# Loading the weights on the rows' queue, a later look at the redo count, and logit columns made by TensorE

## The chip, the cores and the metric

The kernel runs on one core of a Trainium2 chip. The metric is device time in microseconds for one execution; before the change the median of three runs is 2867.93 us (2864.26 to 2868.86). A profile of one execution tells when each instruction started, how long it ran, and what ended the wait before it.

The engines by their names in the profile: PE (TensorE, products; PEld is its loading of weights), DVE (VectorE), ACT (ScalarE), POOL (GpSimd), SP (SyncE, which here issues transfers). Each engine takes its instructions in the order in which they were written, and an instruction that waits holds up those behind it on that engine.

## The reference

Two graph layers over 4096 nodes with 256 features, in float32. Cut to what matters:

```
h   = relu(layernorm(x));  hw = (h @ W) in 4 heads of 64
src = hw . a[:64],  dst = hw . a[64:]              # one logit each per node and head
out = softmax over neighbours of leakyrelu(src_i + dst_j), times hw
x   = x + layernorm(out)
X   = relu(layernorm(x))
for n in 0, 1:
    P  = softmax(X W1' W2' (X W3')')                # 4096 x 4096
    A  = P cut to the smallest set of entries that holds 0.9 of each row, renormalised
    Xf = R Xf;  X = A X                             # R: the graph's adjacency with self loops, normalised
    Z += Xf U1[n]' + X U2[n]'
result = x + layernorm(relu(layernorm(x)) + Z)
```

## The kernel before, in words

The 4096 rows are 32 blocks of 128. The kernel runs in stages.

**Prologue.** `X` holds all rows. SP loads block 0 (L197), blocks 1 to 3 (L201) and then seven groups of four (L195). ACT's queue loads the vector `a` copied to all 128 partitions (`a_r`, L198), the two halves of W into the tile `wx` (L200), then three tiles of weights for the attention layer (L204 to L206). `wx` has 256 columns of W and 8 more. Those 8 are W times the two halves of `a`, per head, so that one product of a row block with `wx` yields both `hw` and the logits. Before the loop over blocks, DVE makes these columns with four multiplications (L571) and four sums (L573), two of each for each half of W. Between the halves it measures mean and variance of blocks 1 to 3 (`measured`, L149 and L150), and after them those of blocks 4 to 7. POOL makes scale and shift from them (`steps`, L141 to L144): for block 0 alone, then for blocks 1 to 3 together, then by fours. `opened` applies them on ACT (`hb`, L240), `turned_rows` transposes on PE (L247), `multiplied` copies the transposed rows to `hT` (ACT, L251) and multiplies with `wx` (PE, L254).

`turn_of(b)` then works one turn for each block: it transposes block b+1, multiplies block b, opens block b+2, measures block b+8, and splits earlier blocks into bfloat16 parts for the masked products that follow (L395). These products are the first long stage of PE; they end near 789 us. The stage after them is the first graph product (L622), with the first attention step's preparation woven in.

**Attention steps.** For each of the two steps n, block b's probabilities `e` are searched by DVE for the cut, and masked (L1022). PE transposes them in eight groups of four (`turn`, L1088, copied to `eT` by ACT at L1090) and sums the chosen rows (`gather`, L1096). `attend` interleaves these eight groups with other work from a table, `beside`, which maps a group number to functions called after that group. `turn` takes its PSUM tile from a pool of two (`tp`).

At the end of a step the kernel must know whether any row's search failed. `questioned` makes the flags after the last block's masking (DVE, L1164 to L1176). `looked` calls `counted`, which sums the flags with two small PE products (L878, in two `tp` tiles) and reads them out on DVE (L880 to L884), and `chosen`, which sorts the numbers of the blocks to redo (DVE, L1192 to L1201). `number` reads the count into a register of every engine (L1187). `repaired` then redoes blocks if the count is above zero. In the kernel before, `looked` stands after group 6 of block 30, and `number` in `beginning`, after group 0 of block 31. In step 0, the last block also carries the loads for the second graph product: `both_weights` (L717) after group 1, `begin` (rows and adjacency, L455 and L474) after group 2.

All waits between engines are semaphores that the compiler of the program places. Transfers from SP and ACT share eight semaphores in turn, so a transfer also waits until the eighth one before it has landed.

Of the kernel before, what the change touches and what calls it, by code (L numbers as in the profile page):

```python
# [11 lines left out]
F32 = mybir.dt.float32  # L12
# [11 lines left out]
AX = mybir.AxisListType  # L24
# [32 lines left out]
def gat_then_top_p_diffusion(  # L57
# [79 lines left out]
    def steps(mv, n, pool, rs=None, nmr=None):  # L137

        if rs is None:
            rs, nmr = (pool.tile([P, n], F32, name=x, bufs=2) for x in (f"rs{n}", f"nmr{n}"))  # L140
        nc.gpsimd.tensor_scalar(rs, mv[:, :, 1], EPS, None, ALU.add)  # L141
        nc.gpsimd.tensor_tensor(rs, rs, mhalf.to_broadcast([P, n]), ALU.pow)
        nc.gpsimd.tensor_scalar(nmr, mv[:, :, 0], -1.0, None, ALU.mult)
        nc.gpsimd.tensor_tensor(nmr, nmr, rs, ALU.mult)  # L144
        return rs, nmr
# [16 lines left out]
    with tc.tile_pool(name="l0", bufs=1) as l0, tc.tile_pool(name="l0s", bufs=2) as l0s, tc.tile_pool(name="l0o", bufs=1) as l0o:  # L162
# [25 lines left out]
        pro = SimpleNamespace(read=lambda: None, hb={}, pt={}, hT={}, pm={}, uv={}, scales={})  # L188
        with tc.manual_schedule(engines=every | {ET.SP}):
            wx = rp.tile([P, KC, D + 2 * H], F32, name="wx", tag="ar", bufs=4)  # L190
            a_r, w1_s, w2_s, w1_r, sT = (rp.tile(sh, F32, name=x, tag="hl", bufs=5) for x, sh in (
                ("a_r", [P, 2 * HD]), ("w1_s", [P, KC, DA]), ("w2_s", [DA, DA]), ("w1_r", [DA, KC, P]), ("sT", [P, P])))

            def block_rows(g):
                nc.sync.dma_start(X[:, ts(g, 4), :], x[ts(g, 4 * P), :].rearrange("(b p) d -> p b d", p=P))  # L195

            nc.sync.dma_start(X[:, 0, :], x[:P, :])  # L197
            nc.scalar.dma_start(a_r, bass.AP(tensor=a.tensor, offset=a.offset, ap=[[0, P], [1, 2 * HD]]))  # L198
            for k in range(KC):
                nc.scalar.dma_start(wx[:, k, :D], w[ts(k, P), :])  # L200
            nc.sync.dma_start(X[:, 1:4, :], x[P:4 * P, :].rearrange("(b p) d -> p b d", p=P))  # L201
            for g in range(1, NB // 4):
                block_rows(g)
# [19 lines left out]
            def measured(b):  # L223
                if b < NB:
                    if b % 4 == 0:
                        pro.mv = l0s.tile([P, 4, nc.vector.BN_AGGR_DIM], F32, name="mv4")
                    moments_of(pro.mv[:, b % 4, :], X[:, b, :])
                    if b == 0:
                        pro.first = [l0s.tile([P, 4], F32, name=f"{x}4") for x in ("rs", "nmr")]
                        steps(pro.mv[:, :1], 1, l0s, *(t[:, :1] for t in pro.first))  # L230
                    if b == 3:
                        steps(pro.mv[:, 1:], 3, l0s, *(t[:, 1:] for t in pro.first))
                    elif b % 4 == 3:
                        pro.scales[b // 4] = steps(pro.mv, 4, l0s)

            def opened(b):
                if b < NB:
                    rs, nmr = pro.scales[b // 4] if b > 3 else pro.first
                    hb = pro.hb[b] = l0s.tile([P, D], F32, name="hb", tag="ob")
                    nc.scalar.activation(hb, X[:, b, :], AF.Relu, scale=rs[:, b % 4:b % 4 + 1], bias=nmr[:, b % 4:b % 4 + 1])  # L240

            def turned_rows(b):
                if b < NB:
                    hb = pro.hb.pop(b)
                    pt = pro.pt[b] = in_bank(3 + b % 2, [P, KC, P])
                    for k in range(KC):
                        nc.tensor.transpose(pt[:, k, :], hb[:, ts(k, P)], ident)  # L247
# [317 lines left out]
        rest.update({5 + i: lambda i=i: factors(i) for i in range(2)})  # L565
        with tc.manual_schedule(engines=every):
            measured(0)
            for k in range(KC):
                for i in range(2):
                    pr = uvs[3 + i][:, :, 0, :HD]  # L570
                    nc.vector.tensor_mul(pr, wx[:, k, :D].rearrange("p (h d) -> p h d", h=H),  # L571
                                         a_r[:, None, ts(i, HD)].to_broadcast([P, H, HD]))
                    nc.vector.reduce_sum(wx[:, k, ds(D + i * H, H)], pr, axis=AX.X)  # L573
                if k == 0:
                    for b in range(1, 4):
                        measured(b)
            for b in range(4, 8):
                measured(b)
            opened(0)
            turned_rows(0)  # L580
            opened(1)
            for b in range(NB):
                turn_of(b)
            read(NB - 1)
            weighed(NB - 1)
            mask_stage(1)
            signed(3)
            sign_stage(2)
            for n, (k, p) in enumerate(todo):
                if n > 0 and p == 0:  # L590
                    later.extend(evacuate(k - 1))
                sign_stage(n + 3)
                mask_stage(n + 2)
                if n == 0:
                    products(k, p, ms[n], range(5))
                    spread_all()
# [589 lines left out]
    def number(R, total):  # L1186
        return nc.values_load(total[1], engines=everyone, min_val=0, max_val=6 * P * NB)  # L1187
# [159 lines left out]
    for n in range(STEPS):  # L1347
# [4 lines left out]
        with tc.manual_schedule(engines=every):  # L1352
# [50 lines left out]
            def beginning():  # L1403
                normal(blocks[NB - 3])
                gathered(blocks[NB - 2])
                finish(blocks[NB - 2])
                finish_scale(blocks[NB - 2])
                R.count = number(R, R.undone)

            beside = {NB - 2: {5: last_chosen, 6: looked}, 0: dict(zip((0, 1, 3, 5, 6), S.turned))}  # L1410
            for b in range(NB - 1):
                chosen_kept(b)
                if b + AHEAD < NB:
# [6 lines left out]
                polished(blocks[NB - 3])  # L1420
                finish_rows(blocks[NB - 2])

            beside = {0: beginning, 3: earlier}
            if n + 1 < STEPS:
                second = hop_of(n + 1)
                beside.update({1: both_weights, 2: lambda: begin(second, 4), 5: lambda: split(second, 2), 6: lambda: (split(second, 4), own(second, 4))})
            attend(r, cur, None, beside)
            for m in range(second.begun if n + 1 < STEPS else 0):
                for s in range(KC):
# [37 lines left out]
```

## Time and profile before

| what | value |
|---|---|
| median of the runs | 2867.93 us |
| profiled execution, its own time | 2866.9 us |
| its span | 2865.1 us |
| PE busy | 2795.3 us, 98% |
| DVE busy | 2169.1 us, 76% |
| ACT busy | 1918.8 us, 67% |
| first product with `wx` (L254) | 14.12 us |
| first masked product (L395) | 88.58 us |
| count of step 0 on PE (L878) | 1776.60 us |
| count of step 1 on PE (L878) | 2834.86 us |
| last store issued (L1304) | 2861.26 us |

A timeline line gives start, duration, engine, source line, instruction, what it writes and reads, and shape; the brackets hold how long its engine was idle before it and what released it. A line "x8" merges eight instructions of a kind. PE shows two records for one float32 product, so the four products of a `gather` are eight records. Lines L1 to L1466 are those of the kernel before.

### The profile page before, as it was taken

To read this page: it belongs to the slowest core of one execution; us is meant where nothing else is said; L and a number is where in the kernel's file an instruction comes from. 1 tells how busy PE (TensorE), PEld (TensorE's weight loads), DVE (VectorE), ACT (ScalarE), POOL (GpSimd) and SP (SyncE) were. 2 spreads that over 40 slices of the span, in tenths; PEclk is the share of its full clock that TensorE was granted. 3 is DMA by queue.
4 is the path that set the end of the run, shared out by engine and by line. 5 is a ranking of instruction groups with operands and counts; after the bars stand their busy time and mean duration, and the time that the engine had idled before them with its cause. 6 is when DMAs were issued, how large, how long until landed. Compare 5 with 4: busy or idle time off the path is not lost. (4 is left out here: it accounts for less than half of the span.)

```text
span 2865.1 us, 51492 instructions
## 1 busy us (share of the span) xinstructions
PE 2795.3 (98%) x18777; PEld 2436.3 (85%) x18777; DVE 2169.1 (76%) x5069; ACT 1918.8 (67%) x3065; POOL 865.7 (30%) x1811
## 2 busy tenths in 40 slices
PE   5999999999999999999999999999999999999998
PEld 4899999999978788888888888667778888888886
DVE  8867868678554385888888887333665999999996
ACT  7876886879543636788878874233627788777882
POOL 6402121010000121222332231000204756666664
PEclk8999999999999999999999999999999999999999
DMA  8969596696376783000000001767991111111110
GB/s 192 243 250 204 204 234 188 229 198 222 133 236 196 240 298 95 20 20 20 27 20 20 20 20 56 229 200 236 327 340 43 31 41 31 31 31 33 39 29 25
DMA packets 190394, 376.48 MB, mean 131 GB/s; under 512 B 18224, under 2 KB 143152, under 8 KB 186032
## 3 DMA queue, kind: packets, MB, share of 16 engines
q1 hardware_dynamic: 146832, 275.05, 29.9%
q0 software_dynamic: 21504, 83.89, 12.3%
q10 hardware_dynamic: 21792, 14.11, 1.6%
q8 instruction: 152, 2.49, 0.4%
q14 instruction: 114, 0.93, 0.1%
HBM read 305.55 MB, written 113.57 MB: 146 GB/s over the span
## 5 line engine op out<-in xcount | busy, mean ns | idle before, releaser
L1096 PE MATMUL acc<-X,eT 128*128 128x256 f32 x4096 | 973.6, 383 | 3.4 <-ACT eT L1090 2.8
L1096 PEld LDWEIGHTS acc<-X,eT 128*128 128x128 f32 x4096 | 739.1, 190 | 111.5 <-ACT eT L1090 31.5
L395 PE MATMUL acc<-ut,m 128*128 128x195 bf16 (+1 forms) x8192 | 698.7, 246 | 2.2 <-DVE st L412 1.7
L395 PEld LDWEIGHTS <-m 128*128 128x128 fp8e4 x8192 | 695.9, 97 | 4.9 <-DVE st L412 2.2
L369 ACT ACTIVATE g<-sr,d_big 128x1024 uint8<-128x1024 f32 x448 | 472.6, 1136 | 3.4 <-DVE m L375 3.4
L911 ACT ACTIVATE e<-mm,nm 128x1024 f32<-128x1024 f32 x256 | 286.1, 1117 | 200.1 <-PE mm L728 198.8
L1090 ACT COPY eT<-tp 128x512 f32<-128x512 f32 x512 | 296.5, 580 | 87.5 <-PE tp L1088 87.4
L997 DVE MAX8 cand<-big 128x8 f32<-128x228 f32 (+1 forms) x1152 | 348.2, 380 | 0.0
L622 PE MATMUL mm<-ar,hl 128*128 128x512 f32 x844 | 340.7, 407 | 5.9 <-ACT ob L502 1.3
L979 DVE SCALAR_TENSOR_TENSOR big<-e,c 128x4096 f32<-128x4096 f32 x58 | 261.9, 4516 | 97.5 <-POOL c L964 67.1
L622 PE MATMUL acc<-ar,hl 128*128 128x512 f32 x844 | 328.6, 392 | 2.3 <-DVE stage L632 1.3
L935 POOL TENSOR_TENSOR sums<-sums 128x2 f32<-128x2 f32 x64 | 12.6, 197 | 1030.9 <-ACT void L918 1030.9
L1088 PE MATMUL tp<-ident,e 128*128 128x128 f32 x2048 | 306.0, 272 | 0.8 <-DVE e L1022 0.8
L1088 PEld LDWEIGHTS tp<-ident,e 128*128 128x128 f32 x2048 | 254.8, 140 | 60.2 <-PE acc L1106 1.2
L375 DVE TENSOR_TENSOR m<-g,ax 128x512 uint32<-128x512 uint32 x256 | 180.8, 706 | 109.9 <-PE acc L395 91.4
L1022 DVE SCALAR_TENSOR_TENSOR e<-e,found 128x4096 f32<-128x4096 f32 x58 | 259.1, 4468 | 0.0
L918 ACT ACTIVATE void<-e,c1x 128x2048 int8<-128x2048 f32 x128 | 257.4, 2011 | 0.8 <-ACT stage L651 0.8
L918 ACT ACTIVATE void<-e,c 128x2048 int8<-128x2048 f32 x128 | 257.5, 2012 | 0.0
L728 PE MATMUL mm<-kT,qT 128*128 128x512 f32 x512 | 198.4, 468 | 2.9 <-ACT e L911 1.9
L376 DVE TENSOR_TENSOR m<-m,ax 128x512 uint32<-128x512 uint32 x256 | 180.4, 705 | 26.0 <-PE acc L395 0.9
L622 PEld LDWEIGHTS mm<-ar,hl 128*128 128x128 f32 x844 | 158.6, 188 | 44.9 <-issue 5.0
L622 PEld LDWEIGHTS acc<-ar,hl 128*128 128x128 f32 x844 | 158.6, 188 | 39.9 <-issue 4.9
(302 smaller groups left out, 3507.4 us busy)
## 6 DMA issues: line engine op xcount, KB each, us to landing
ar<-adj_d SPq DMA_DIRECT2D x211, 512.0 KB, 4.7
adj_d<-ax POOLq DMA_DIRECT2D x32, 2048.0 KB, 7.7
ut<-uv_d SPq DMA_DIRECT2D x60, 784.0 KB, 5.6
aru<-adj_d SPq DMA_DIRECT2D x45, 512.0 KB, 4.6
ax<-in_adj_t_dram POOLq DMA_DIRECT2D x32, 512.0 KB, 17.4
x<-xf_d SPq DMA_DIRECT2D x78, 128.0 KB, 4.9
xf<-xft_d SPq DMA_DIRECT2D x64, 128.0 KB, 2.3
sr<-s_d SPq DMA_DIRECT2D x15, 512.0 KB, 4.9
```

Source lines behind the costliest of these rows:

```text
L369: nc.scalar.activation(g[:, c, :], shared[k].sr, AF.Relu, scale=BIG, bias=d_big[:, h, j:j + 1])
L395: nc.tensor.matmul(shared[k].acc[i][:, t, :cols], m[t][:, c, ts(i, P)], shared[k].ut[j // QUARTER][:, j % QUARTER, t, :cols], start=(j == ...
L622: nc.tensor.matmul(A.acc[c][s], A.hl[m][:, t, ts(s, P)], A.ar[m][:, ts(c, 512)], start=(j == 0 and t == 0), stop=(j == NB - 1 and t == 1))
L728: nc.tensor.matmul(pm[:, h, :], q[t], kT[:, ds(h * (N // 2) + c * 512, 512)], start=(t == 0), stop=(t == 1))
L911: nc.scalar.activation(ev[:, :, c, :], r.pm[c], AF.Exp, bias=r.nm, accum_out=r.sums[:, c // 2, c % 2:c % 2 + 1])
L918: nc.scalar.activation(void, r.e[:, ts(h, N // 2)], (AF.Relu, AF.Sign)[i], bias=r.c1, scale=-1.0, accum_out=r.sums[:, h, 2 + i:3 + i])
L979: nc.vector.scalar_tensor_tensor(big, r.e, r.c3, r.e, ALU.is_le, ALU.mult, accum_out=r.low3)
L997: nc.vector.max(cand[:, s, :], big[:, edges[s]:edges[s + 1]])
L1022: nc.vector.scalar_tensor_tensor(r.e, r.e, r.t, r.e, ALU.is_ge, ALU.mult, accum_out=kept)
L1088: nc.tensor.transpose(pt[:, i, :], r.e[:, ts(4 * g + i, P)], ident)
L1090: nc.scalar.copy(eT, pt)
L1096: nc.tensor.matmul(r.acc[:, 0, :], eT[:, i, :], cur[:, j, :], start=(j == 0), stop=(j == NB - 1))
```

## The change

It has three parts. W is loaded in one transfer on SP's queue, behind block 0 and ahead of blocks 1 to 3, and ACT's queue loads `a` into a tile `spots` instead: zero but for the entries of `a`, each put at its own row of W' and in the column of its head and half. The 8 columns of `wx` are then made by PE: four transposes of W's quarters, copied by DVE to `w_t`, and four products of `w_t` with `spots`, copied by DVE into `wx`. Blocks 1, and 2 with 3, get their scales separately. Finally `looked` goes to group 1 of block 31, the reading of the count to group 4 (`asked`), and `both_weights` to group 2, ahead of `begin`.

```diff
-            a_r, w1_s, w2_s, w1_r, sT = (rp.tile(sh, F32, name=x, tag="hl", bufs=5) for x, sh in (
-                ("a_r", [P, 2 * HD]), ("w1_s", [P, KC, DA]), ...
+            w_t, w1_s, w2_s, w1_r, sT = (rp.tile(sh, F32, name=x, tag="hl", bufs=5) for x, sh in (
+                ("w_t", [P, KC, KC, P]), ("w1_s", [P, KC, DA]), ...
             nc.sync.dma_start(X[:, 0, :], x[:P, :])
-            nc.scalar.dma_start(a_r, bass.AP(tensor=a.tensor, offset=a.offset, ap=[[0, P], [1, 2 * HD]]))
-            for k in range(KC):
-                nc.scalar.dma_start(wx[:, k, :D], w[ts(k, P), :])
+            spots = l0.tile([P, KC, 2, H], F32, name="spots")
+            nc.vector.memset(spots, 0.0)
+            for h in range(H):
+                nc.scalar.dma_start(spots[ds(h * HD % P, HD), h * HD // P, :, h],
+                                    bass.AP(tensor=a.tensor, offset=a.offset, ap=[[1, HD], [HD, 2]]))
+            nc.sync.dma_start(wx[:, :, :D], w.rearrange("(k p) d -> p k d", p=P))
             nc.sync.dma_start(X[:, 1:4, :], x[P:4 * P, :].rearrange("(b p) d -> p b d", p=P))
...
-                        steps(pro.mv[:, :1], 1, l0s, *(t[:, :1] for t in pro.first))
+                    if b < 2:
+                        steps(pro.mv[:, ds(b, 1)], 1, l0s, *(t[:, ds(b, 1)] for t in pro.first))
                     if b == 3:
-                        steps(pro.mv[:, 1:], 3, l0s, *(t[:, 1:] for t in pro.first))
+                        steps(pro.mv[:, 2:], 2, l0s, *(t[:, 2:] for t in pro.first))
...
             measured(0)
+            pt = in_bank(0, [P, KC, KC, P])
             for k in range(KC):
-                for i in range(2):
-                    pr = uvs[3 + i][:, :, 0, :HD]
-                    nc.vector.tensor_mul(pr, wx[:, k, :D].rearrange("p (h d) -> p h d", h=H),
-                                         a_r[:, None, ts(i, HD)].to_broadcast([P, H, HD]))
-                    nc.vector.reduce_sum(wx[:, k, ds(D + i * H, H)], pr, axis=AX.X)
-                if k == 0:
-                    for b in range(1, 4):
-                        measured(b)
+                for c in range(KC):
+                    nc.tensor.transpose(pt[:, k, c, :], wx[:, k, ts(c, P)], ident)
+            nc.vector.tensor_copy(w_t, pt)
+            opened(0)
+            turned_rows(0)
+            pm = in_bank(1, [P, KC, 2 * H])
+            for k in range(KC):
+                for c in range(KC):
+                    nc.tensor.matmul(pm[:, k, :], w_t[:, k, c, :], spots[:, c].rearrange("p t h -> p (t h)"),
+                                     start=(c == 0), stop=(c == KC - 1))
+            for b in range(1, 4):
+                measured(b)
+            nc.vector.tensor_copy(wx[:, :, D:], pm)
             for b in range(4, 8):
                 measured(b)
-            opened(0)
-            turned_rows(0)
             opened(1)
...
                 finish_scale(blocks[NB - 2])
+
+            def asked():
                 R.count = number(R, R.undone)
 
-            beside = {NB - 2: {5: last_chosen, 6: looked}, 0: ...}
+            beside = {NB - 2: {5: last_chosen}, 0: ...}
...
-            beside = {0: beginning, 3: earlier}
+            beside = {0: beginning, 1: looked, 3: earlier, 4: asked}
             if n + 1 < STEPS:
                 second = hop_of(n + 1)
-                beside.update({1: both_weights, 2: lambda: begin(second, 4), 5: ..., 6: ...})
+                beside.update({2: lambda: (both_weights(), begin(second, 4)), 5: ..., 6: ...})
```

More of the change, by code (lines that the diff above doesn't have):

```diff
@@ L190, in gat_then_top_p_diffusion @@
             wx = rp.tile([P, KC, D + 2 * H], F32, name="wx", tag="ar", bufs=4)
-            a_r, w1_s, w2_s, w1_r, sT = (rp.tile(sh, F32, name=x, tag="hl", bufs=5) for x, sh in (
-                ("a_r", [P, 2 * HD]), ("w1_s", [P, KC, DA]), ("w2_s", [DA, DA]), ("w1_r", [DA, KC, P]), ("sT", [P, P])))
+            w_t, w1_s, w2_s, w1_r, sT = (rp.tile(sh, F32, name=x, tag="hl", bufs=5) for x, sh in (
+                ("w_t", [P, KC, KC, P]), ("w1_s", [P, KC, DA]), ("w2_s", [DA, DA]), ("w1_r", [DA, KC, P]), ("sT", [P, P])))
             def block_rows(g):
@@ L1407, in beginning @@
                 finish_scale(blocks[NB - 2])
+            def asked():
                 R.count = number(R, R.undone)
-            beside = {NB - 2: {5: last_chosen, 6: looked}, 0: dict(zip((0, 1, 3, 5, 6), S.turned))}
+            beside = {NB - 2: {5: last_chosen}, 0: dict(zip((0, 1, 3, 5, 6), S.turned))}
             for b in range(NB - 1):
@@ L1421, in earlier @@
                 finish_rows(blocks[NB - 2])
-            beside = {0: beginning, 3: earlier}
+            beside = {0: beginning, 1: looked, 3: earlier, 4: asked}
             if n + 1 < STEPS:
                 second = hop_of(n + 1)
-                beside.update({1: both_weights, 2: lambda: begin(second, 4), 5: lambda: split(second, 2), 6: lambda: (split(second, 4), own(second, 4))})
+                beside.update({2: lambda: (both_weights(), begin(second, 4)), 5: lambda: split(second, 2), 6: lambda: (split(second, 4), own(second, 4))})
             attend(r, cur, None, beside)
```

## The prediction

> **What bounds the kernel now.** I read first the page's busy times, then the busy time by stretches, then the timeline around the three places that the diff touches: the first 16 us, the end of the first attention step, and the last 40 us.
>
> ```profile
> PE 2795.3 (98%) x18777; PEld 2436.3 (85%) x18777; DVE 2169.1 (76%) x5069; ACT 1918.8 (67%) x3065; POOL 865.7 (30%) x1811
> ...
> 20.00:30.00 10.00, 6.93 (x34) 4.88 (x32) 9.46 (x30) 9.21 (x27) 7.50 (x11) 1.00 0.39 86
> 30.00:40.00 10.00, 7.12 (x28) 5.35 (x28) 9.86 (x30) 8.67 (x26) 8.33 (x15) 0.83 1.02 175
> ...
> 100.00:120.00 20.00, 20.00 (x238) 20.00 (x237) 18.93 (x26) 18.62 (x22) 10.36 (x11) 1.00 0.99 196
> ```
>
> The first line is the page's (engine, busy us, share); the others give, by stretch, PE, PEld, DVE, ACT and POOL busy time, then clock, DMA share and GB/s. PE is busy 98% of the span, and from 100 us almost without a gap. So an edit pays only where PE waits, or where the work ahead of PE's long run (the prologue, bound by DVE at 9.5 to 9.9 us of each 10) starts late. Time gained before such a stretch is kept, because what follows is a queue of work and no fixed date.
>
> The timeline of the first 16 us (start, duration, engine, line, what; in brackets the idle time before and what ended it):
>
> ```profile
> 4.33 0.43 DVE L149 BATCH_NORM_STATS2 st<-X 128x6 f32<-128x256 f32 x1 [4.33 <-DMA X<-in_x_dram]
> ...
> 7.69 0.43 DVE L571 TENSOR_TENSOR sr<-wx,a_r 128x256 f32<-128x256 f32 x1 [2.72 <-DMA wx<-in_w_dram]
> ...
> 8.24 0.60 ACT L240 ACTIVATE hb<-X,nmr,rs 128x256 f32<-128x256 f32 x1 [6.21 <-DMA X<-in_x_dram]
> ...
> 11.05 0.31 POOL L141 TENSOR_SCALAR rs<-mv 128x3 f32<-128x3 f32 x1 [4.53 <-DVE mv L150]
> ...
> 12.98 0.60 ACT L240 ACTIVATE hb<-X,nmr,rs 128x256 f32<-128x256 f32 x1 [4.14 <-POOL nmr L144]
> ...
> 14.12 1.97 PE L254 MATMUL b<-wx,hT 128*128 128x264 f32 x4
> ```
>
> PE's first product (14.12) hangs on hb of row block 1 (12.98), that on POOL's factors (11.05), and those on DVE having measured blocks 1 to 3, which it did behind four of the L571/L573 instructions.
>
> The timeline at the ends of the two attention steps:
>
> ```profile
> 1773.44 1.89 PE L1096 MATMUL acc<-X,eT 128*128 128x256 f32 x8
> 1776.60 0.22 PE L878 MATMUL tp<-undone,ones 128*1 128x32 f32 x2 [1.27 <-DVE undone L1176]
> ...
> 2829.65 1.89 PE L1096 MATMUL acc<-X,eT 128*128 128x256 f32 x8
> 2834.86 0.27 PE L878 MATMUL tp<-undone,ones 128*1 128x32 f32 x2 [3.32 <-DVE undone L1176]
> ...
> 2835.17 3.44 PE L1096 MATMUL acc<-X,eT 128*128 128x256 f32 x8
> ```
>
> PE stands at the count (L878) until DVE has the flags: 1.27 and 3.32 us. After the longer stand the next eight products take 3.44 instead of 1.89 us.
>
> **What the Trainium skill says.** "TensorE: Matmul & The Clock Gate", section "What's actually happening": PE falls to half clock after an idle window of about 3.4 us; the 3.44 us group fits that (the short stand shows no slow group). "DMA: Bandwidth & Descriptors", section "Rules for kernel authors": an access whose last dimension is not contiguous becomes one descriptor per element; each of the four spread loads is 128 pieces of 4 bytes, and no row of this trace has such. Same page, "Issuing engines are not separate DMA queues": changing the queue saves only issue time. The trace differs here: from 5 to 6 us SP's queue has 81% of DMA time and ACT's 17%, and wx, issued on ACT at 1.21, lands 6.4 to 7.3 us later. Position decides.
>
> **The prologue.** Removed: eight DVE instructions of 0.39 to 0.43 us, 3.4 us, and the 64 KB row of a. Added: a small memset, four loads of 0.5 KB, four PE transposes, four PE products with 8 columns, a DVE copy of 128x512 (0.69 us, the L782 row) and one of 128x16 (about 0.15), and four short POOL operations, as block 1 gets factors of its own.
>
> Arrival. SP's queue has moved 0.13 MB at 3 us, 0.41 at 5, 0.66 at 6, 0.93 at 7. Transfers are signalled 1.3 us (block 0) to 2.4 us (blocks 1 to 3) after their bytes. W is now second: 0.39 MB, so bytes at 4.9 and signal at 6.2 to 7.3; I take 6.7. Blocks 1 to 3 go behind it: 0.77 MB, bytes at 6.4, signal at 7.7 to 8.8 (before: 7.79); I take 8.4. ACT still issues the key weights ahead of hb, and by the built kernel's waits the last of them (L206 before, issued at 7.80) waits for blocks 1 to 3: hb of block 0 starts at about 8.85 instead of 8.24.
>
> Two paths to the first product.
> - By block 1: W at 6.7, four cold transposes (two took 0.69 at 8.89) to 7.9, DVE copy to 8.65, block 1 measured (0.43+0.18) by 9.25, POOL's four steps (5.06 to 6.52 for one column, 1.46) to 10.7, hb at 10.8; before, the product came 1.14 after hb's start: 11.95.
> - By the columns: hb of block 0 to 9.45, its transposes to 10.2, then the spread products queued behind them. The nearest row, L827 (65 columns, 16 records in 1.73 us warm), gives 0.108 a record, so 0.9 us warm and 1.7 cold for eight records; I take cold: 11.9. Then DVE's copy to 12.1 and block 1's transposes to 12.6.
>
> The later one sets it: 12.6 instead of 14.12, 1.5 us. Bounds 0 (W as late as before) and 3 (early W, warm PE). Blocks 4 to 7 are measured behind the column copy, until 14.2; their factors are ready at 16.2, hb of block 4 by 16.85, and PE, 1.5 us earlier, wants it at 17.8: hidden, but with only 1 us of room. The rows of later blocks come behind 0.25 MB more, with many us to spare. The small loads must land by about 10; issued from 1 to 3 us and nearly empty, I put them at 5 to 7.
>
> **The count.** The two L878 products move from before the last eight products of block 30 to after the second gather of block 31; flags are then long ready (2834.5 against PE there at about 2838.7). Block 31's masked rows are ready at 2830.9 and PE now asks for them at 2833.6, so no new stand there. What it costs: L878 takes a pair of the two rotating buffers that the transposes use, so the next transposes wait until DVE has read the count out. Before, L878 started at 1776.60 and that reading ended at 1777.31; before, eight products covered it. Now nothing does: 0.9 us each step with the pair itself.
> First step: PE's weight loads are free at 1774.93, the gather came at 1776.81: 1.9 - 0.9 = 1.0 us. Last step: free at 2831.14 and, unhindered, 1.60 later at the next group (2832.74), where it was 2838.23: 5.5 - 0.9 = 4.6 us.
>
> The reading of the count into registers moves from the last block's group 0 to group 4 on all engines. "DMA: Bandwidth & Descriptors", "Latency and other measured facts", prices a tensor load at about 0.6 us; here L1187 takes 0.3 to 0.6. On PE it lies under queued products (before, no gap at the transposes behind it, 2842.47; 1.9 us of cover), on POOL before the last factors (6.0 us idle), on DVE in 14.1 us of idle time. On SP it was ahead of the second weights and hop loads (u issued at 1782.41 after 0.9 us); now it is behind them, and ahead of an aru load that waits for PE until 1798 anyway. If these covers were gone it would be 0.6 us per step. The chain after the first step (xa stored, rows loaded, first ar) starts at the last block's end and moves along. DVE's second half for block 30 now follows the count; its store has over 10 us.
>
> Sum: 1.5 + 1.0 + 4.6 = 7.1 us. The profiled execution, 2866.9 with a span of 2865.1, would be 2859.8 and 2858.0; the median of the runs, 2867.93, is 1.0 above it, so I forecast 2860.8.
>
> **Rivals.**
> - The prologue gives nothing: W and the rows arrive together late, or hb of block 4 is short of its 1 us. For it: only 1 us of cover, and bytes that stay the same. Against: block 1 no longer waits for 2 and 3. 5.6 us, 2862.3.
> - The wait returns at the transposes behind L878: if DVE is behind there by 2 us per step instead of 0.9, and PE stays cool at the end (1.5), 3.5 us are lost: 2864.3. Against: DVE's last work before it ends at about 2836, 2.5 us before PE comes.
> - Slower: the columns of the logits are now rounded otherwise; if a single row then fails the top-p test, a block is redone. Nothing is redone before: nothing runs after the last store at 2861.26. Price from rows: 8 column groups of about 0.6 (ACT, half of 1.117 each), six passes or half passes over 4096 columns (about 14), eight groups of 2.17: at least 36 us, about 2900. It decides from the first row on.
> - The move does nothing, if PE needs the masked rows as late as the flags: excluded by 2830.9 against 2834.5.
>
> **Numbers.** Forecast 0.64, first rival 0.20, second 0.09, slower 0.04, nothing 0.03. Here 0.2% is 5.7 us, about what a measurement of this kernel can tell from no change. The forecast's own range is 3.5 to 10.5 us of gain, most of it beyond 5.7; the first rival is split about evenly; the others are same or slower. Faster 0.68, same 0.26, slower 0.06. The range takes in the first two rivals and the bounds of the prologue: 2856 to 2866.
>
> **What will show it.** L878 with no wait on DVE, the group after it at 1.9 us, and a short gap (0.5 to 1.0) at the transposes behind; the last gather near 2847.5 instead of 2854.6; first L254 near 12.6 and not 14.1, and the first L395 (88.58) as much earlier. I am wrong if the small loads land after 10 us, if the gain at the first L254 is gone at the first L395, or if new work follows the last store.

## The result and the profile after

The kernel after takes 2859.86 us (median of 8 runs, 2857.15 to 2860.89), the kernel before beside it 2865.49 us (8 runs, 2863.33 to 2868.86). The medians differ by 5.6 us. The ratio estimated from all runs is 0.9977, with a 95% interval of 0.9968 to 0.9987: 6.6 us faster, between 3.7 and 9.2. The profiled execution takes 2860.89 us with a span of 2859.1, against 2866.9 and 2865.1 before.

The first line of the kernel after's page, and its busy times by stretches (columns as in the prediction):

```profile
PE 2798.3 (98%) x18789; PEld 2438.7 (85%) x18789; DVE 2167.1 (76%) x5064; ACT 1919.8 (67%) x3065; POOL 870.5 (30%) x1815
...
30.00:40.00 10.00, 7.66 (x31) 5.85 (x32) 9.86 (x30) 8.66 (x26) 8.51 (x13) 0.84 0.91 181
100.00:120.00 20.00, 20.00 (x238) 20.00 (x237) 18.17 (x25) 18.64 (x20) 8.40 (x9) 1.00 0.91 239
```

PE has 12 more records and 3.0 us more to do; its gaps shrank. What bounds each stretch is as before: DVE, busy 90 to 99% of each 10 us from 20 to 90 us, then PE. The timeline of the first 16 us of the kernel after:

```profile
2.96 0.43 DVE L149 BATCH_NORM_STATS2 st<-X 128x6 f32<-128x256 f32 x1 [2.07 <-DMA X<-in_x_dram]
...
4.76 1.09 PE L575 MATMUL b<-ident,wx 128*128 128x128 f32 x4 [4.76 <-DMA wx<-in_w_dram]
...
6.24 0.60 ACT L244 ACTIVATE hb<-X,nmr,rs 128x256 f32<-128x256 f32 x1 [4.22 <-DMA X<-in_x_dram]
...
9.31 1.42 PE L582 MATMUL b<-spots,w_t 128*128 128x8 f32 x6 [1.50 <-DMA spots<-in_a_dram]
...
11.09 2.10 PE L258 MATMUL b<-wx,hT 128*128 128x264 f32 x4
```

The first product with `wx` (now L258) starts at 11.09 instead of 14.12. The weights are there at 4.7, and even block 0, whose load was not touched, comes 1.4 us earlier. What comes last is a small load: PE waits 1.50 us for `spots`. The first masked product (now L399) starts at 85.59 instead of 88.58, so in these two traces the 3 us are kept until there.

The timeline at the ends of the attention steps (L1096 is now L1104, L878 is L886, the transposes L1096):

```profile
1771.31 3.62 PE L1104 MATMUL acc<-X,eT 128*128 128x256 f32 x16
1781.05 0.22 PE L886 MATMUL tp<-undone,ones 128*1 128x32 f32 x2
1781.82 0.66 PE L1096 MATMUL tp<-ident,e 128*128 128x128 f32 x4 [0.49 <-DVE ns_i_u L892]
...
2827.58 3.62 PE L1104 MATMUL acc<-X,eT 128*128 128x256 f32 x16
2837.32 0.22 PE L886 MATMUL tp<-undone,ones 128*1 128x32 f32 x2
2838.14 0.66 PE L1096 MATMUL tp<-ident,e 128*128 128x128 f32 x4 [0.55 <-DVE ns_i_u L892]
```

The sixteen products run through (3.62 us) where PE stood 1.27 and 3.32 us. L886 waits for nothing; behind it PE stands 0.49 and 0.55 us until DVE has read out the sums. Matched instruction by instruction, the traces show the lead of the kernel after over the kernel before: ahead of the end of step 0 it is 2.1 us and behind it 3.0; ahead of the end of step 1 it is 2.1 and behind it 6.4. So the ends gave 0.85 and 4.4 us. With the 3.0 of the prologue that is 8.2; the spans differ by 6.0. So about 2 us net were lost in between, above all in the two graph products (985 to 1005 and 2025 to 2112 us), where nothing was changed.

### The profile page after: what moved, and what is told of

Its sections match the earlier page's. It is cut to its first block, busy times and chain, and to the rows that moved or that the text cites. A ratio compares the mean times of both kernels' runs of the same rounds, so it can differ in the third digit from the quotient of the medians.

```text
span 2859.1 us, 51521 instructions
## 1 busy us (share of the span) xinstructions
PE 2798.3 (98%) x18789; PEld 2438.7 (85%) x18789; DVE 2167.1 (76%) x5064; ACT 1919.8 (67%) x3065; POOL 870.5 (30%) x1815
## 5 line engine op out<-in xcount | busy, mean ns | idle before, releaser
L1104 PE MATMUL acc<-X,eT 128*128 128x256 f32 x4096 | 971.7, 382 | 3.4 <-ACT eT L1098 2.8
L1104 PEld LDWEIGHTS acc<-X,eT 128*128 128x128 f32 x4096 | 738.2, 190 | 111.2 <-ACT eT L1098 31.7
L399 PE MATMUL acc<-ut,m 128*128 128x195 bf16 (+1 forms) x8192 | 698.7, 246 | 1.9 <-DVE st L416 1.4
L399 PEld LDWEIGHTS <-m 128*128 128x128 fp8e4 x8192 | 695.9, 97 | 4.6 <-DVE st L416 1.8
L1096 PE MATMUL tp<-ident,e 128*128 128x128 f32 x2048 | 306.1, 272 | 1.9 <-DVE ns_i_u L892 1.0
L1096 PEld LDWEIGHTS tp<-ident,e 128*128 128x128 f32 x2048 | 254.8, 140 | 61.2 <-DVE ns_i_u L892 1.3
```

What stands on the lines that cost most here:

```text
L399: nc.tensor.matmul(shared[k].acc[i][:, t, :cols], m[t][:, c, ts(i, P)], shared[k].ut[j // QUARTER][:, j % QUARTER, t, :cols], start=(j == ...
L1096: nc.tensor.transpose(pt[:, i, :], r.e[:, ts(4 * g + i, P)], ident)
L1104: nc.tensor.matmul(r.acc[:, 0, :], eT[:, i, :], cur[:, j, :], start=(j == 0), stop=(j == NB - 1))
```

## The experiments

The theory I started with (A): each gain is local, is kept, and they add up. The rival (B): the graph products take an earlier start back, because their transfers set the pace there. (In the second one DMA moves 348 GB/s at a share of 0.99, in the first 216 GB/s at 0.70; PE is busy 96% of both.) Further questions were what makes the start of the prologue earlier, and what still holds it.

**The two parts alone.** The first kernel undoes the count's part (the reading of the count goes back into `beginning`), the second makes only that.

```diff
 # e1, against the kernel after
-            beside = {NB - 2: {5: last_chosen}, ...
+            beside = {NB - 2: {5: last_chosen, 6: looked}, ...
-            beside = {0: beginning, 1: looked, 3: earlier, 4: asked}
+            beside = {0: beginning, 3: earlier}
-                beside.update({2: lambda: (both_weights(), begin(second, 4)), ...
+                beside.update({1: both_weights, 2: lambda: begin(second, 4), ...
 # e2: the same lines, the other way round, against the kernel before
```

> The kernel after with the count's part undone: only the prologue differs from the kernel before. Theory A (each gain is local and is kept): the first L258 product starts near 11.1 us as in the kernel after (14.12 before), the first attention group (L399) about 3.0 us earlier than before, and the count still stands 1.3 and 3.3 us for DVE with a slow group after the second stand; time 3.0 us below the kernel before, ratio 0.9990. Theory B (the graph products, whose stretches move 340 to 350 GB/s and are bound by DMA, take an earlier start back): the 3.0 us shrink to about 2 behind the first graph product (near 1000 us) and to 1 or less behind the second (near 2110), time 0 to 1.5 us below. The prediction's own step was 1.5 us, with a first product at 12.6.

> The kernel before with the count's part alone: the prologue is that of before. Theory A: first product at 14.1 us, no shift until the end of attention step 0; there 0.85 us gained, at the end of step 1 another 4.4, time 5.2 us below the kernel before, ratio 0.9982; the group of sixteen L1096 products around the count at 3.6 us both times. Theory B: the 0.85 us of step 0 is gone behind the second graph product, time 4.4 below. If the slow group of before was not caused by the 3.32 us stand, a group near 3.4 for eight products stays and the gain at the last step is about 2.8 instead of 4.4.

Measured beside the same runs of the kernel before (2866.31 us): the prologue alone 2864.2, ratio 0.9993 (0.9985 to 1.0002), so 2.0 us; the count alone 2861.78, ratio 0.9985 (0.9978 to 0.9991), so 4.3 us. Together 6.3, where the kernel after has 6.6. The sum fits, within intervals 3.7 to 4.9 us wide. The first interval holds no change too: that the prologue's part gains rests on the traces below and is not shown by the times.

At the end of step 1 the kernel with the prologue alone has the stand of before, but not what followed it. Timelines of this kernel, and of the kernel before in a second run (its expectation comes further down):

```profile
2833.53 0.22 PE L886 MATMUL tp<-undone,ones 128*1 128x32 f32 x2 [3.32 <-DVE undone L1184]
...
2833.74 1.99 PE L1104 MATMUL acc<-X,eT 128*128 128x256 f32 x8
```

```profile
2834.58 0.27 PE L878 MATMUL tp<-undone,ones 128*1 128x32 f32 x2 [3.30 <-DVE undone L1176]
...
2834.89 3.52 PE L1096 MATMUL acc<-X,eT 128*128 128x256 f32 x8
```

After a stand of 3.32 us the eight products took 1.99, after one of 3.30 they took 3.52 (3.44 in the first trace of the kernel before, after 3.32). What differs is where the stand falls. Within each trace the granted clock changes only at whole multiples of 3.413 us from one another: before, half clock begins at 69.92, 80.16 and 2834.72 us, which are 3 and 807 of them apart. So the time of a trace is cut into windows of 3.41 us. The two windows at the stand (columns as above; the sixth figure behind the length is the clock), first of the kernel before, then with the prologue alone:

```profile
2831.30:2834.72 3.42, 0.24 (x2) 0.00 (x0) 3.07 (x12) 0.00 (x0) 1.93 (x4) 1.00 0.00 0
2834.72:2838.13 3.41, 3.27 (x11) 2.65 (x12) 2.56 (x19) 0.00 (x0) 0.00 (x0) 0.50 0.00 0
```

```profile
2828.69:2832.10 3.41, 1.52 (x8) 0.99 (x6) 3.17 (x11) 0.47 (x1) 3.12 (x5) 1.00 0.00 0
2832.10:2835.52 3.42, 1.99 (x12) 1.78 (x13) 2.61 (x18) 0.00 (x0) 0.00 (x0) 1.00 0.00 0
```

Before, the stand fills nearly a whole window (PE busy 0.24 us of it, 0.12 in the second run), and the next window runs at half clock. With the prologue alone an edge cuts the stand in two (PE busy 1.52 and 1.99 us), and the clock stays. The Trainium skill, "TensorE: Matmul & The Clock Gate", section "What's actually happening", says that the window of about 3.4 us is free-running and does not start anew with the kernel; these three traces agree. So about 1.5 of the 4.4 us come in some executions and not in others, with the place of the windows.

**What makes the start earlier.** Block 0 is measured from 4.33 us before and from 2.96 after; in every trace without the load of `a_r` it came by 3.4. Two kernels ask whether that load is the cause, a third, with the weights ahead of the small loads on ACT's queue, whether the queue is.

```diff
 # e10, against the kernel before
-            nc.scalar.dma_start(a_r, bass.AP(tensor=a.tensor, offset=a.offset, ap=[[0, P], [1, 2 * HD]]))
             for k in range(KC):
                 nc.scalar.dma_start(wx[:, k, :D], w[ts(k, P), :])
+            nc.scalar.dma_start(a_r, bass.AP(tensor=a.tensor, offset=a.offset, ap=[[0, P], [1, 2 * HD]]))
 # e11, against the kernel before
-            nc.scalar.dma_start(a_r, bass.AP(tensor=a.tensor, offset=a.offset, ap=[[0, P], [1, 2 * HD]]))
+            nc.scalar.dma_start(a_r, w[:P, :2 * HD])
 # e6, against the kernel after
+            for k in range(KC):
+                nc.scalar.dma_start(wx[:, k, :D], w[ts(k, P), :])
-            nc.sync.dma_start(wx[:, :, :D], w.rearrange("(k p) d -> p k d", p=P))
```

> The kernel before with one line moved: the row of a, spread over 128 partitions (64 KB), is loaded behind the two halves of the weights on ACT's queue instead of ahead of them. Theory C (that load holds up all that goes with it: in every run without it row block 0 is there by 2.8 to 3.4 us, in the two with it at 4.1 and 4.3): block 0 is measured from 2.9 to 3.4, the weights land at 3.7 to 5 as in the run with the weights first on ACT's queue, and the row of a comes near 7, so that the first L571 starts at 6.5 to 7.2 instead of 7.2 to 7.7. Rival (the sum of bytes in flight sets the landings): block 0 still at 4.1 or later, weights at 6 or later.

> The kernel before, with the row of a replaced by a piece of the weights of the same size and shape in the tile (128 partitions of 512 B, 64 KB), read from 128 different places instead of 128 times from one. It leaves the attention vector a out, so the logits are other ones and rows may be done again later; only the first 16 us are read. Theory C1 (reading one place of 512 B 128 times is what is slow): block 0 is measured from 2.8 to 3.4, and the weights land at 4.5 to 5.5 instead of 7.2 to 7.7. Theory C2 (64 KB more in the first place of the queue, whatever they hold): block 0 at 4.1 or later and the first L571 at 7.2 or later, as before.

> The kernel after, but the weights go back to ACT's queue, in two transfers of 128 KB ahead of the four small loads; everything else stays. Theory A (the place behind 128 KB on SP's queue is what brings the weights early): they land at 7 to 8.5 us as in the kernel before, not at 4.7, the small loads land later than 9.2 too, and the first L258 starts at 12.5 to 13.5 instead of 11.1; time 1.0 to 2.0 us above the kernel after, ratio to before 0.998 to 0.9985. Rival (the queue only saves issue time, as the Trainium skill's page on DMA, section on issuing engines, has it): the weights land within 1 us of 4.7 and the first L258 within 0.5 us of 11.1.

The transfers issued in the first 14 us (what, queue, size, and in the last column us from issue to landing): first the kernel before, then `a_r` behind the weights, then `a_r` from other addresses.

```profile
wx<-in_w_dram ACTq DMA_DIRECT2D x2, 128.0 KB, 6.8
...
a_r<-in_a_dram ACTq DMA_DIRECT2D x1, 64.0 KB, 4.7
```

```profile
wx<-in_w_dram ACTq DMA_DIRECT2D x2, 128.0 KB, 3.3
...
a_r<-in_a_dram ACTq DMA_DIRECT2D x1, 64.0 KB, 8.5
```

```profile
wx<-in_w_dram ACTq DMA_DIRECT2D x2, 128.0 KB, 4.9
...
a_r<-in_w_dram ACTq DMA_DIRECT2D x1, 64.0 KB, 2.6
```

The same 64 KB in the same place of the queue take 4.7 us when 128 partitions read one place of 512 B, and 2.6 us when they read 128 places; the weights behind come 1.9 us earlier with it. Put behind the weights, the repeated reading takes 8.5 us and the weights land 3.3 us after their issue. It slows the other queue too: block 0, on SP's queue, is measured from 4.33 with it ahead, 3.55 with it behind, 3.17 with other addresses. So C1 holds and C2 falls, on one run each. The 128 places lie in another tensor (`w`); one place of another tensor, read 128 times, was not tried, and why the repeated reading is slow stays open. The first L571 of the run with `a_r` behind starts at 10.32, not at 6.5 to 7.2 as I expected: I had thought that the load only delays others, while it is itself slow. That kernel's first product comes at 16.75 and its first masked one at 90.92 us; its time is 2867.3, beside 2867.12. The kernel with other addresses leaves the attention vector out, so it redoes rows and takes 4320.62 us; only its first 16 us are used here.

With other addresses, and all the arithmetic of before, the timeline reads

```profile
5.31 0.43 DVE L571 TENSOR_TENSOR sr<-wx,a_r 128x256 f32<-128x256 f32 x1 [1.50 <-DMA wx<-in_w_dram]
...
11.74 1.97 PE L254 MATMUL b<-wx,hT 128*128 128x264 f32 x4
```

In the three traces with the prologue of before (both of the kernel before, and the count alone) the first L254 starts at 14.12, 13.98 and 13.60, in the four with the new one (the kernel after, the prologue alone, one buffer, and the count read at once) at 11.09, 10.88, 11.62 and 11.04: 13.90 and 11.16 on average, 2.7 us apart. 2.2 of these are there without any work for PE. The other 0.6 us are what is left for the columns made by PE and the new order of loads; the four traces differ among themselves by 0.7, so this share is not shown.

The queue does not decide when the weights land. With them on ACT's queue, the timeline has the first of their transposes early (those of the second half start at 4.82) and hb late:

```profile
3.69 0.66 PE L576 MATMUL b<-ident,wx 128*128 128x128 f32 x2 [3.69 <-DMA wx<-in_w_dram]
...
11.00 1.09 ACT L245 ACTIVATE hb<-X,nmr,rs 128x256 f32<-128x256 f32 x2 [8.98 <-DMA w_s<-in_w_t_dram]
```

The weights land as early there as on SP's queue (theory A had 7 to 8.5, the rival within 1 us of 4.7; the rival was right on this). But the first product starts at 14.21 and the first masked one at 88.66, so the prologue's gain is gone, in another way than either theory had it. ACT's last weights for the attention layer are issued at 10.35 instead of 5.82, and hb of block 0 stands behind these issues until 11.00. The trace tells which semaphore held them: the load ahead of that one, issued at 9.81, waits for the semaphore of the first group of four row blocks on SP's queue, which landed at 9.80; in the kernel after, the same load waits for that of W, at 4.62. With other transfers in front, the turn of the eight shared semaphores had moved on. The time is 2863.69, ratio 0.9988 (0.998 to 0.9997).

**What still holds the start.** Two kernels take the four small loads to two (with four DVE copies), one of them with the next edit as well; a third also loads block 1 by itself ahead of the weights; a fourth computes the scales of blocks 1 to 3 together again.

```diff
 # e4, against the kernel after (e5: e4 and e3 together)
-            for h in range(H):
-                nc.scalar.dma_start(spots[ds(h * HD % P, HD), h * HD // P, :, h],
-                                    bass.AP(tensor=a.tensor, offset=a.offset, ap=[[1, HD], [HD, 2]]))
+            a_c = l0.tile([P, 2], F32, name="a_c")
+            for i in range(P // HD):
+                nc.scalar.dma_start(a_c[ds(i * HD, HD), :], bass.AP(tensor=a.tensor, offset=a.offset, ap=[[1, HD], [HD, 2]]))
             measured(0)
+            for h in range(H):
+                rows_ = ds(h * HD % P, HD)
+                nc.vector.tensor_copy(spots[rows_, h * HD // P, :, h], a_c[rows_, :])
 # e9, against e5
+            nc.sync.dma_start(X[:, 1, :], x[P:2 * P, :])
             nc.sync.dma_start(wx[:, :, :D], w.rearrange("(k p) d -> p k d", p=P))
-            nc.sync.dma_start(X[:, 1:4, :], ...
+            nc.sync.dma_start(X[:, 2:4, :], ...
 # e7, against the kernel after
-                    if b < 2:
-                        steps(pro.mv[:, ds(b, 1)], 1, l0s, ...)
+                        steps(pro.mv[:, :1], 1, l0s, ...)
-                        steps(pro.mv[:, 2:], 2, l0s, ...)
+                        steps(pro.mv[:, 1:], 3, l0s, ...)
```

> The kernel after, but a is loaded by two small transfers in place of four into a tile of two columns, and four tiny DVE copies spread it. If the last of the four small loads (issued at 3.6 us, landed near 9.2) sets the first product, as the trace's wait at the products with 8 columns says (1.50 us), then these products start at 7.9 to 8.3 instead of 9.31 and the first L258 at 10.0 to 10.3 instead of 11.09: 0.8 us below the kernel after. Rival: the path by row block 1 (hb at 8.69, then its transposes) or DVE, which the four copies delay, is as late: first L258 at 10.8 to 11.1 and a gain under 0.3 us.

> As the last one, and row block 1 (128 KB) is loaded by itself ahead of the weights, blocks 2 and 3 behind them. In the trace with two loads the first L258 product waited for hb of block 1, and that for the one landing of blocks 1 to 3 at 7.26 us. If that is what sets it, block 1 lands near 4, the weights near 5.3 instead of 4.5, and the products with 8 columns set the start: first L258 at 9.6 to 10.0 instead of 10.61. Rival: the prologue's end is set by DVE and ACT, busy 97% from 30 us on, and keeps under 0.3 us of it: time within 0.3 us of the last one.

> The kernel after, but the scales of row blocks 1 to 3 are computed together again, when all three have been measured, as in the kernel before. The three blocks land together, so block 1's scales wait for two more measurements on DVE (0.61 us each): hb of block 1 starts 1.0 to 1.5 us later than 8.69. If hb of block 1 is as late as the columns (first L258 came 0.14 us behind the copy of the columns in the kernel after), the first L258 starts at 11.8 to 12.5 instead of 11.09, and 0.3 to 1.0 us is left of it at the first L399. Rival: the products with 8 columns, which wait for the small loads, hide it and the first L258 stays at 11.1 to 11.4.

The timeline with two loads:

```profile
6.58 1.88 PE L585 MATMUL b<-spots,w_t 128*128 128x8 f32 x8
...
9.47 0.60 ACT L244 ACTIVATE hb<-X,nmr,rs 128x256 f32<-128x256 f32 x1 [3.72 <-POOL nmr L144]
...
10.61 1.97 PE L258 MATMUL b<-wx,hT 128*128 128x264 f32 x4
```

The products with `spots` come 2.7 us earlier, the first L258 only 0.5: half theory, half rival. Now block 1 is last. Loading it first didn't help (first L259 at 10.93), because DVE measures it behind the copy of `w_t`; the timeline of that kernel:

```profile
6.86 0.69 DVE L580 COPY w_t<-b 128x512 f32<-128x512 f32 x1 [1.91 <-PE b L579]
7.58 0.43 DVE L149 BATCH_NORM_STATS2 st<-X 128x6 f32<-128x256 f32 x1
```

So hb of block 1 starts at 9.79: I had moved the load but not the measuring. With the scales together again hb of block 1 starts at 10.00 instead of 8.69, as expected, and the first product at 11.13: the late small loads hide it (the rival), so the change's separate scales brought nothing yet. This is one run, of 2857.97 us.

The first masked product starts at 88.58, 88.47 and 87.61 with the prologue of before, at 85.59, 86.31, 86.08 and 85.49 with the new one: 2.35 us of the 2.7 are left there. The two loads alone have it at 85.51, with the one buffer as well at 84.96, and with block 1 first at 85.27. A start 0.5 us earlier is lost among differences of 0.8 us between kernels with one and the same prologue.

**The pause behind the count.** One kernel splits `totals` into the product and the reading out, and puts both sums into one `tp` tile, so that the transposes find the other one free; another reads the count into registers right behind its products.

```diff
 # e3, against the kernel after
-        R.undone, R.failed = totals(R.undone, "u"), totals(R.failed, "f")
...
+        pt = ps2.tile([P, 4, P], F32, name="tp")
+        totals(R.undone, "u", pt[:, 0, :])
+        totals(R.failed, "f", pt[:, 1, :])
+        R.undone, R.failed = read_out("u", pt[:, 0, :]), read_out("f", pt[:, 1, :])
 # e8, against the kernel after
-            beside = {0: beginning, 1: looked, 3: earlier, 4: asked}
+            beside = {0: beginning, 1: lambda: (looked(), asked()), 3: earlier}
```

> The kernel after, but both sums of the count lie in one buffer of the rotating pair, so that the transposes behind take the other one. If the 0.49 and 0.55 us in which PE stands at those transposes come from the pair being taken (the prediction's step: 0.9 us per step with the products themselves), the transposes start without a wait on DVE's read-out, 0.5 us earlier in each step: 1.0 us below the kernel after, ratio to before about 0.9974. Rival: the transposes wait for their own input on DVE just as long (exponentials that are released late), then the wait changes its name, keeps 0.3 us or more, and the gain is under 0.3 us.

> The kernel after, but the count is read into the engines' registers right behind its products (after the second gather), not three groups further on. The prediction priced the loss of the cover at 0.6 us per step. Theory A: PE stands behind the two L886 products until DVE has written the count and the register is loaded (0.3 to 0.6 us by the L1187 rows), so the pause there grows from 0.5 to between 1.0 and 1.5 us in each step; 1 to 2 us in all. Rival: the products queued on PE cover it and the pause stays at 0.5.

The transposes behind the count at the end of step 1, first with one buffer, then with the reading at once (timeline):

```profile
2837.26 0.66 PE L1098 MATMUL tp<-ident,e 128*128 128x128 f32 x4
```

```profile
2837.82 0.63 PE L1096 MATMUL tp<-ident,e 128*128 128x128 f32 x4 [0.80 <-DVE n_i_f L890]
```

With one buffer the pause is gone in both steps: the taken pair was its cause. From the sixteen products around the old place of the count to the next such group, at the last block's end, it is 19.97 us instead of 20.58. The time, 2860.17 and a ratio of 0.9978 (0.997 to 0.9987), doesn't show so little. The reading at once makes the pauses 0.91 and 0.80 instead of 0.49 and 0.55: 0.4 and 0.25 us, less than both the 0.6 of the prediction and the 0.5 to 1.0 of the expectation. The one run with it took 2860.71 us.

**Both edits together.**

> The kernel after with both of the earlier edits: one buffer for both sums of the count, and two small loads of a with four DVE copies. If the gains of the traces add up (0.5 to 0.6 us at each step's end; first L258 at 10.6 instead of 11.1, of which 0.2 to 0.5 is left at the end of the prologue), the time is 1.3 to 1.7 us below the kernel after: ratio to before 0.9970 to 0.9973. If the low median of the two loads alone (ratio 0.9967) was worth what it said, it is 0.9963 or lower; its trace shows no place for that.

It takes 2854.78 us, ratio 0.9963 (0.995 to 0.9977), the fastest of all; with block 1 first 2856.81, ratio 0.9969 (0.9957 to 0.9981); the two loads alone 2857.13, ratio 0.9967 (0.9955 to 0.9979). All three intervals hold the 0.9970 to 0.9973 that the traces' gains add up to, and also the ratio of the kernel after; they do not decide between the two cases of the expectation either, though 0.9963 is the figure of its second. That it is faster than the kernel before is shown; that it beats the kernel after is likely from the traces and not shown by the times. Single executions mislead here: from 100 us to PE's last product, the trace with both edits has no window at half clock, that of the kernel after one, that of the two loads alone three, and this last execution, 2861.91 us, is the slowest of its six runs (the others take 2855.57 to 2857.37).

**The 2 us that were lost on the way.**

> The kernel before once more, unchanged, for a second look at its trace. If the slow group of eight products (3.44 us) at the end of the last attention step is a fixed effect of the 3.32 us stand, it is there again. If the clock falls only in some executions (with the prologue's part alone the same stand was followed by a group of 1.99), it may be either; the stand itself is 3.3 us again. Block 0 is measured from 4.1 to 4.4 and the first L254 starts at 13.4 to 14.2. The stretches 780 to 1005 and 2025 to 2112 us, which the change does not touch, differ from the first look by up to 1.5 us of PE idle time, if the 2 us that the kernel after lost there are spread from execution to execution.

The second run of the kernel before (2866.77 us) has a lead of 2.3 us over the first at 2025 us and of only 0.4 at 2112, with no edit at all. The kernel after goes from 3.9 to 2.2 in the same stretch. PE's idle time there does not tell them apart: it is 3.5 us in the first run of the kernel before, 3.8 in the second, 3.6 in the kernel after, and 2.2 to 4.4 in the others. The clock does. A window at half clock in the kernel after, and one in the second run of the kernel before:

```profile
2101.70:2105.12 3.42, 3.42 (x9) 2.62 (x8) 3.26 (x6) 0.41 (x1) 0.00 (x0) 0.50 0.98 330
```

```profile
2104.15:2107.57 3.42, 3.42 (x10) 2.65 (x9) 3.35 (x5) 0.81 (x2) 0.00 (x0) 0.50 1.04 397
```

In both traces PE waits for a tile of the adjacency just before it (1.81 and 2.50 us). In the first trace of the kernel before it waits too (2.23 us), and no slow window follows. The window takes 1.6 us of the lead in each: from 3.75 to 2.16 in the kernel after and from 2.0 to 0.4 in the second run, nearly all that was lost there. In the first graph product, from 985 to 1005 us, every other trace loses 0.2 to 1.5 us against the first one of the kernel before, its own second run 0.7, the kernel after 0.8: there it was the first trace that was quick.

Nor do the leads behave as theory B says. Of the traces without a slow window from 2025 to 2112 us, the count alone goes from a lead of 0.3 to 1.3 there, the prologue alone from 2.5 to 1.7, both edits from 6.4 to 8.0: the largest lead was not taken back. The kernel with `a_r` behind the weights, 2.3 us late at the first masked product, is still 2.0 late at 2800 us. (At the last count it stands 1.63 us, no slow window follows, and its span ends only 0.4 us above that of the first trace.) But single traces wander by a microsecond or more (the one with the weights on ACT's queue loses 1.4 us from 2025 to 2112 of a lead of 0.2), and of the prologue alone's lead, 2.8 us at 780, only 1.4 is there at 2800. So the idea that the graph products take an earlier start back as a rule is not borne out; that they take a part of it is not excluded.

## Why the prediction was right, and where it was not

The time is 2859.86 where 2860.8 was forecast, and the gain of 3.7 to 9.2 us holds the 7.1. That the time came so close is partly luck: the forecast started from 2867.93, the median of three runs, and eight runs gave 2865.49. Whether the gain is above the 0.2% (5.7 us) to which the prediction gave 0.68 is open, as the interval lies on both sides of it. Step by step:

- **Arrival: wrong, and in both directions.** The weights were put at 6.7 and the rows at 8.4; they came at 4.7 and before 6.2. The step took the slow first 5 us of SP's queue from the trace of before as a property of the queue, and it was an effect of the very load that the change removes. The two busy shares from 1.5 to 4.5 us say so, before and after (queue 1 is SP's, queue 10 ACT's; packets, MB, share):

```profile
q1 hardware_dynamic: 306, 0.30, 36.7%
q10 hardware_dynamic: 211, 0.13, 21.9%
```

```profile
q1 hardware_dynamic: 702, 0.68, 77.1%
q10 hardware_dynamic: 144, 0.00, 2.6%
```

  In the same 3 us the two queues used 59% of the engines' time before and 80% after. Before, the engines had time to spare while transfers landed late; I should have asked what kept them.
- **"Position decides": wrong.** The prediction set the Trainium skill's sentence aside ("DMA: Bandwidth & Descriptors", section "Issuing engines are not separate DMA queues": another queue saves only issue time). With the weights on ACT's queue they landed just as early (3.7 and 4.8 us, 4.7 on SP's); the sentence stood. What ACT's queue cost was its issue order ahead of hb, with the semaphores on which its issues wait.
- **Small loads at 5 to 7 us: wrong.** The last landed near 9.2 us, and PE waited 1.50 us for it. The prediction had named landing after 10 us as what would make it wrong. The rule that it quoted from "DMA: Bandwidth & Descriptors", section "Rules for kernel authors", one descriptor per element, fits: in the first 14 us the packets under 512 B rise from 767 to 1316, and to 1036 with two loads. Each small load takes ACT 0.6 to 0.7 us to issue, where the issue of the a row took 0.4.
- **The path by the columns sets the first product: right, for another reason.** Not hb of block 0 behind the key weights, but `spots` was late. It starts at 11.09 instead of 12.6. The prologue's term, 1.5, measured 2.7 us at the first product and 2.35 at the first masked product; it lay within the bounds of 0 to 3. "Kept until the first masked product" was right but for these 0.35 us. Block 4's cover of 1 us held in effect: no loss there was to be seen.
- **The count, step 0: right.** 1.0 forecast, 0.85 measured.
- **The count, step 1: right in size.** 4.6 forecast, 4.4 measured, but about 1.5 of it is not there in each execution: once of three times the same stand was cut by the edge of a window and left the clock at full speed. The prediction took it as certain.
- **The pause behind the pair of buffers: right.** 0.9 us with the products was 0.77 and 0.82, and one buffer removed it.
- **The reading of the count hidden at group 4: right.** Without the cover it costs 0.25 to 0.4 us, not 0.6.
- **Rivals.** The prologue did give something, by the traces; the wait didn't return beyond 0.55 us; no row was done again (the last store is issued at 2854.84 and no work follows it). "The move does nothing" was rightly left out. The second rival's loss, twice 1.1 and 1.5, adds up to 3.7, not 3.5.

Two errors of the arrival step partly cancelled: early rows and weights, late small loads. Measured term by term the gains are 3.0, 0.85 and 4.4, 8.2 us, and about 2 of these are missing in the span, 1.6 of them through one window at half clock. The total was close for the count's terms, and partly by luck for the prologue's.

## What to carry to other kernels

A resource that looks slow in the trace of before may be slow because of what the change takes away; when the queues leave the engines time to spare (41% here) and transfers still land late, look for one transfer that is itself slow. Here a small load of scattered elements landed 3.4 to 6.6 us after its issue and held the issue order of its engine; two loads spread by DVE brought the products behind them 2.7 us forward. Where PE's stand is about as long as the clock's window, count the slow products behind it as possible and not as certain. And before two single traces are compared, their windows at half clock should be counted: in these traces one was worth about 1.6 us.

## What I had not expected

Reading one row of 512 B into 128 partitions took 4.7 us (8.5 behind other transfers) where 128 different pieces took 2.6, and it slowed a transfer on the other queue by 1.2 us. And the unchanged kernel wanders by 2.3 us in the middle of its span between two executions whose spans differ by 0.2 us: 1.6 of these us go again in one window at half clock behind a short wait. A matched comparison of two single traces, however exact, says little about gains of a microsecond or two in such stretches.
